# Column sums of 18 more attention groups on VectorE instead of TensorE, later folds, and quotients issued singly

## The chip, the core and the metric

The kernel runs on one core of a Trainium2 chip. A core has five engines with a queue of instructions each: TensorE (PE: matmuls, and PEld, its weight loads), VectorE (DVE), ScalarE (ACT), GpSimd (POOL) and SyncE (SP, which here issues DMAs). Each engine takes its own queue in order, and waits at an instruction until the semaphores that it names are set. The metric is the device time of one execution in microseconds (us). Before the change it is 3623.77 us, the median of 3 runs from 3623.32 to 3624.26.

## What is computed

Two attention layers over `x` of 8 x 32 x 32 x 512 (float32), each behind a group norm of 32 groups and with a residual. Layer 0 has 16 heads of 32, layer 1 has 4 heads of 128 and a bias from relative positions. Cut to what matters:

```python
def attention_layer_0(xn):                     # per batch: 1024 tokens x 512
    q, k, v = split(xn @ w_qkv)                # 16 heads of 32
    attn = softmax(einsum('bhid,bhjd->bhij', q * 32 ** -0.5, k), axis=-1)
    out = einsum('bhij,bhjd->bhid', attn, v)
    return merge(out) @ w_proj + b_proj

def attention_layer_1(xn):                     # 4 heads of 128
    scores = (xn @ Wq * 128 ** -0.5) @ (xn @ Wk).T + relative_positions
    return merge(softmax(scores) @ (xn @ Wv)) @ Wo

x = x + attention_layer_0(_gn(x))
x = x + attention_layer_1(_gn(x))
```

The softmax of layer 0 is what the change is about: the exponentials are multiplied with `v` first, and the result is divided by the sum of the exponentials afterwards.

## The kernel before

**Stages.** All work is in `quick_path` (L30). The kernel walks over the 8 batches and overlaps them. In stage b, `attention_0` of batch b (L859) is the leading strand, and `side_by_side` (L1611) places beside each of its steps some of the "rest": the output projection of layer 0 for batch b-1, that of layer 1 for batch b-2, the projections and the attention of layer 1 for batch b-1 (`attention_1`), loads, and the projections of layer 0 for batch b+1 (`before_0`). `side_by_side` counts costs in units of PE work, so that the rest is spread evenly over the 64 steps of the leading strand. `woven` (L1599) does the same on a smaller scale: it puts one step of a side strand after chosen steps of a main strand. Each strand is a Python generator, and a `yield` ends a step. The order written so is what a scheduler starts from when the program is built; it fixes the order of each engine's queue. `tc.issue_after(ins)` asks for an instruction not to be queued ahead of another, and `tc.keep_in_program_order` is for matmuls that may not be moved.

**Projections.** Matrix products with the weights are done with seven products in place of eight (`seven`, L506), with matmuls in four column strips of 32 (`by_columns`, L426, matmul L430). The names `x_`, `y_`, `z_` are its PSUM banks, and `a_`, `b_`, `p_` the partial results that ACT copies and DVE adds (L520, L528, L682, L685). `reader[0]`, `begun[0]` and `half_done[0]` hold the latest of certain adds, to which other work is tied.

**Attention of layer 0.** A batch has 8 groups: m (a set of 4 heads, in the order 0, 2, 1, 3) times h (a half of 512 queries). A group has 8 steps j over blocks of 128 keys:

- `front` (L878): 8 matmuls (L886) into the PSUM tile `ps`, four banks wide, of which there is one; then one exponential on ACT (L901) of 128 x 2048 elements into a slot of `e_room`.
- `back` (L904), one step behind: 4 matmuls (L912) add e times v into `acc`, and, but for the first step, DVE adds e to the group's running sum `esum` (L924).

`e_room` has three slots. Two take turns for the exponentials; the third holds the sum of the group, for which the first exponential's own slot is used. So the slot of the old group's sum is freed for exponentials when the group is finished, and the third exponential of the new group (j = 2) writes into it.

The 128 partitions of `esum` still have to be added up. There are two ways:

- `finish` (L930): four matmuls with `ones` (L934, 512 columns each) give the sums over partitions, spread over the strip; ACT copies them to SBUF (L764), DVE transposes in blocks of 32 (L766), takes the reciprocal (L781), checks it (L784) and spreads it by another transpose (L796); POOL multiplies `q` (where `acc` was put) with it (L770).
- `Apart` (L807): DVE transposes each of the four 512-column parts of `esum` (L826) and reduces each by 32 (L829) into a slot of `few_0`. Transposes 3 and 4 are tied behind `reader[0]`. For a tuple of groups, one `fold_up` (L837) of four small matmuls (L841) adds what is left, DVE inverts it, and each group has a `quotient`: a spread (L796) and POOL's multiplication (L857).

Which groups go the second way is told by `APART` (L26) and `apart_of` (L138): none in batch 0, (2, 3) in batch 1, (2, 3, 4) in batches 2 to 6, (3, 4) in batch 7. The tuple (2, 3, 4) is handed to the attention of layer 1 that runs beside it, which folds it with its own sums (`closing`) and issues its quotients among its own (`quotients`, woven into `before_0`).

**Attention of layer 1** (`attention_1`) has its scores by L1139, exponentials by L1142, its products by L1153 and adds on DVE (L1167, L1169); it has the sums of all its groups folded at once and its 8 quotients issued in pairs, each followed by one of `aside_0`.

Of the kernel before, what the change touches and what calls it, by code (L numbers as in the profile page):

```python
# [22 lines left out]

BLOCKS = 8

APART = [(2, 3, 4)]  # L26


@with_exitstack
def quick_path(  # L30
# [107 lines left out]
    def apart_of(b):  # L138
        if b == 1:
            return [(2, 3)] + APART[1:]  # L140
        return [] if b == 0 else [(3, 4)] if b == B - 1 else APART

    n_checks = B * CC * NH + 2 * 4 + B - 2
    n_checks -= sum(len(some) - 1 for b in range(B) for some in apart_of(b))
# [650 lines left out]
    def spread(su, rec):  # L795
        return nc.vector.transpose(  # L796
            su.rearrange("p (t c) -> p t c", c=32),
            rec.unsqueeze(2).to_broadcast([P, NB // 32, 32]),
        )
# [2 lines left out]
    e_room = mem.tile([P, 3, HB, NB], F32, tag="e0", name="e_room", bufs=1)  # L802
    turn, sum_at = [0, 1], [2]

    few_0 = mem.tile([P, HB, 3, NB // 32], F32, tag="few0", name="few_0", bufs=1)

    class Apart:  # L807


        def __init__(self, b, some):  # L810
            self.b, self.some = b, some
            self.groups = []
            self.width = len(some) * (NB // 32)

        def place(self, r):
            return few_0[:, r, : len(self.some), :]

        def take(self, m, h, esum, dst):
            at = len(self.groups)
            self.groups.append((m, h, dst))  # L820
            for r0 in range(0, HB, 2):
                turned = []
                for r in (r0, r0 + 1):
                    t = mem.tile([P, NB], F32, tag="rec", name=f"tu_0_{self.b}_{m}_{h}_{r}", bufs=2)
                    with tc.issue_after(reader[0].ins) if r0 else nullcontext():
                        nc.vector.transpose(t, esum[:, r, :])  # L826
                    turned.append(t)
                for r, t in zip((r0, r0 + 1), turned):
                    nc.vector.tensor_reduce(  # L829
                        few_0[:, r, at, :],  # L830
                        t.rearrange("p (t c) -> p t c", c=32),
                        axis=AX.X,
                        op=ALU.add,
                    )
                yield
# [16 lines left out]
        def quotient(self, i, behind=None):  # L852
            m, h, dst = self.groups[i]
            su = mem.tile([P, NB], F32, tag="rec", name=f"su_0_{self.b}_{m}_{h}", bufs=2)
            with tc.issue_after(behind.ins) if behind is not None else nullcontext():
                spread(su, few_0[:, 0, i, :])
            nc.gpsimd.tensor_tensor(dst, dst, su, op=ALU.mult)  # L857

    def attention_0(q, k, v, b, blocks=range(NT)):  # L859

        steps = [(m, h, j) for m in (0, 2, 1, 3) for h in range(NH) for j in blocks]
        state = {}
        aparts = {i: part for some in apart_of(b) for part in [Apart(b, some)] for i in some}

        def sums_apart(i, m, h, esum):
            part = aparts[i]
            together = i == 4 and b < B - 1
            if together:
                aside.append(part)
            yield from part.take(m, h, esum, q[m][:, h * NB : (h + 1) * NB])  # L870
            if together or i != part.some[-1]:
                return
            part.fold_up()
            for i in range(len(part.some)):
                yield
                part.quotient(i)

        def front(m, h, j):  # L878
            name = f"0_{b}_{m}_{h}_{j}"
            ps = wide_tile(f"ps_{name}")  # L880
            for i in range(2):

                some = slice(64 * i, 64 * i + 64)
                for r in range(HB):
                    rows = slice(r * D0, (r + 1) * D0)
                    nc.tensor.matmul(  # L886
                        ps[some, r, :],
                        k[m][rows, j * P + 64 * i : j * P + 64 * i + 64],
                        q[m][rows, h * NB : (h + 1) * NB],
                        start=True,  # L890
                        stop=True,
                    )
            at = turn.pop(0)
            if j == blocks[0]:

                turn.append(sum_at[0])
                sum_at[0] = at
            else:
                turn.append(at)
            e = e_room[:, at]  # L900
            exps[0] = nc.scalar.activation(e, ps, AF.Exp, scale=D0 ** -0.5)  # L901
            return e

        def back(m, h, j, e):  # L904
            name = f"0_{b}_{m}_{h}_{j}"
            if j == blocks[0]:
                state["acc"] = psum.tile([P, NB], F32, tag="acc", name=f"acc_{name}", bufs=1)
                state["first"] = e
            acc = state["acc"]
            for r in range(HB):  # L910
                c0 = (m * HB + r) * D0
                nc.tensor.matmul(  # L912
                    acc[r * D0 : (r + 1) * D0, :],
                    v[:, j, c0 : c0 + D0],
                    e[:, r, :],
                    start=(j == blocks[0]),
                    stop=(j == blocks[-1]),
                )
            if j == blocks[1]:
                state["esum"] = state["first"]  # L920
            if j != blocks[0]:

                with tc.issue_after(reader[0].ins) if beside_norm[0] else nullcontext():
                    summed[0] = nc.vector.tensor_add(state["esum"], state["esum"], e)  # L924
            if j != blocks[-1]:
                return
            nc.scalar.copy(q[m][:, h * NB : (h + 1) * NB], acc)
            state["ended"] = (m, h, state["esum"])

        def finish(m, h, esum):  # L930
            name = f"0_{b}_{m}_{h}"
            su = psum.tile([P, NB], F32, tag="acc", name=f"sums_{name}", bufs=1)
            for r in range(HB):
                nc.tensor.matmul(  # L934
                    su[r * D0 : (r + 1) * D0, :],
                    ones,
                    esum[:, r, :],
                    start=True,
                    stop=True,
                )  # L940
            normalise(q[m][:, h * NB : (h + 1) * NB], su, name)

        pending = None
        ended, ending = 0, []
        for at in steps:
            if "ended" in state:
                if ended in aparts:
                    ending.append(sums_apart(ended, *state.pop("ended")))
                else:
                    finish(*state.pop("ended"))  # L950
                ended += 1
            for part in ending:
                next(part, None)
            e = front(*at)
            if pending is not None:
                back(*pending)
            pending = (*at, e)
            yield 2
        for part in ending:
            run(part)  # L960
        back(*pending)
        yield 1
        finish(*state.pop("ended"))
# [113 lines left out]
    def attention_1(q, k, v, seeds, b, beside=0, final=False):  # L1077
# [161 lines left out]
            yield 0  # L1239

        def quotients():
            for i in range(H1 * NH):
                late = half_done if i // 2 % 2 == 0 else closed
                run(quotient(i, late[0], nc.gpsimd))
                if i % 2:
                    if aside_0 is not None and i // 2 < len(aside_0.some):
                        aside_0.quotient(i // 2, begun[0])
                    yield 0

        ends.append(closing())  # L1250
        if together:
# [347 lines left out]
    def woven(main, side, start, gap, places=(0,)):  # L1599

        for at, cost in enumerate(main):
            if at >= start and (at - start) % gap in places:
                cost += next(side, 0)
            yield cost
        yield from side

    def run(part):
        for _ in part:
            pass
# [36 lines left out]
    def later(part, *args):  # L1646

        yield from part(*args)
# [48 lines left out]
    for b in range(B + 1):  # L1697
# [69 lines left out]
        if coming is not None:  # L1767

            before = later(before_0, b + 1, coming, forms_0 if last is not None else None)
            if b + 2 < B:  # L1770
                n = len(ORDER)
                turning = later(turn_ahead, b + 2, states[b + 2], int(last is None))
                before = woven(before, turning, *((n - 1, n, (0, 4)) if last is None else (2 * n + 3, n, (0, 3))))
            if last is not None:
                before = woven(before, later(left.pop), 3, len(ORDER), (0, 3))
            rest.append(before if last is not None else woven(before, other_sums(), 2, 7))
            total += 3 * PRODUCT - PRODUCT // 2
        if b == 0:
# [502 lines left out]
```

## Time and profile before

| | |
|---|---|
| median of 3 runs | 3623.77 us (3623.32 to 3624.26) |
| the profiled execution, own time | 3626.2 us |
| its span, first to last instruction | 3624.4 us |
| mean granted TensorE clock | 0.999 |
| exponentials of layer 0 (L901) | 512 of 1879 ns |
| adds into the sum (L924) | 448, 2236 to 3393 ns, median 2292 |
| matmuls with `ones` (L934) | 360 in 45 groups, 51.2 us busy |
| fold matmuls (L841) | 56 in 7 folds, 192 to 230 ns |
| POOL's multiplications behind a fold (L857) | 19 of 3122 ns |
| POOL's multiplications behind `finish` (L770) | 45 of 1563 ns |

How the views are read: the first part of the page gives each engine's busy time, its share of the span and its instructions. The chain that ended last follows the work back from the last instruction to what released it. The groups by line have, in this order, the line, engine, operation, what it writes and reads, the count, the busy time and the mean of one in ns, and the idle time of the engine just before them with what ended it. The timeline has the start, the length, and in brackets the idle time before and its releaser. Neighbouring matmuls overlap in their records, so their starts tell more than their lengths.

The busy time of DVE, in stretches of 15 us around the ends of the sixth (1534.1 us) and seventh group (1573.6 us) of batch 3, is 12.90 (from 1515), 10.43, 14.98, 9.35, 11.99 and 11.60 us (to 1605). PE is busy 15.00 us in each.

### The profile page before, as it was taken

The page shows a single profiled execution, that of the slowest core. Times are in us where ns is not written, and L with a number is a line of the kernel's source. Part 1 is how long each engine was busy: PE and PEld are TensorE (multiplying, and loading weights), DVE is VectorE, ACT ScalarE, POOL GpSimd, SP SyncE. Part 2 cuts the span into 40 slices and gives each one's busy share as a digit, 9 for nine tenths or more (in the row PEclk, how much of TensorE's full clock was granted, in tenths as well). Part 3 has the DMA queues.
Part 4 walks back from the last instruction along what each step waited for, and adds up shares of the span by engine and source line. Part 5 has one row for each costly group of instructions (what it writes and reads, how often), then busy time and mean ns, then how long its engine had stood idle before and what let it go on. Part 6 is the DMA issues. An engine that isn't in the chain of part 4 may idle for free.

```text
span 3624.4 us, 80755 instructions
## 1 busy us (share of the span) xinstructions
PE 3604.8 (99%) x33786; PEld 1230.2 (34%) x33786; DVE 2573.9 (71%) x2807; ACT 1990.6 (55%) x2266; POOL 1399.2 (39%) x880
## 2 busy tenths in 40 slices
PE   9999999999999999999999999999999999999999
PEld 4232244232433234332343323433234232323343
DVE  6788656787667966679666796667966678667546
ACT  3555666446664466544665446654566545656254
POOL 1343055231552316523075230742318312166255
PEclk9999999999999999999999999999999999999999
DMA  6233164242643426344363433624336133324376
GB/s 192 73 111 104 44 175 137 64 145 68 187 126 89 131 66 195 110 112 112 84 195 90 135 97 101 186 74 139 85 101 203 55 101 79 103 91 158 97 200 155
DMA packets 577316, 431.96 MB, mean 119 GB/s; under 512 B 274320, under 2 KB 467632, under 8 KB 575920
## 3 DMA queue, kind: packets, MB, share of 16 engines
q1 hardware_dynamic: 567952, 411.05, 40.7%
q0 software_dynamic: 2608, 13.70, 1.0%
q8 instruction: 268, 4.39, 0.5%
q10 hardware_dynamic: 6384, 1.97, 0.2%
q14 instruction: 104, 0.85, 0.1%
HBM read 334.30 MB, written 92.27 MB: 118 GB/s over the span
## 4 chain that ended last, share of the span: by engine, by line
PE 96%; DVE 2%; ACT 1%; issue 1%; DMA 0%; POOL 0%; SPq 0%; DVEq 0%; ACTq 0%; POOLq 0%
PE ps L886 15%; PE acc L912 14%; PE ps L1139 12%; PE acc L1153 12%; PE y_v L430 5%; PE y_q L430 4%; PE y_k L430 4%; PE z_v L430 3%; PE x_v L430 3%; PE z_q L430 3%; PE x_k L430 3%; PE x_q L430 3%; PE z_k L430 3%; PE y_wp L430 2%; PE y_wo L430 2%; PE x_wp L430 2%
## 5 line engine op out<-in xcount | busy, mean ns | idle before, releaser
L901 ACT ACTIVATE e_room<-ps 128x2048 f32<-128x2048 f32 x512 | 962.0, 1879 | 749.8 <-PE ps L886 728.1
L924 DVE TENSOR_TENSOR e_room<-e_room 128x2048 f32<-128x2048 f32 x448 | 1093.4, 2441 | 375.2 <-ACT e_room L901 373.7
L1064 POOL TENSOR_TENSOR pos<-pos,columns 128x512 f32<-128x512 f32 x448 | 642.8, 1453 | 179.5 <-DMA pos<-pr 178.0
L886 PE MATMUL ps<-q,k 32*64 32x512 f32 x8192 | 594.0, 613 | 2.1 <-ACT e_room L901 2.0
L912 PE MATMUL acc<-e_room,v 128*32 128x512 f32 x4096 | 546.8, 604 | 0.0
L1139 PE MATMUL ps<-q,k 128*128 128x512 f32 x1024 | 527.3, 598 | 0.3 <-ACT ps L1073 0.3
L1153 PE MATMUL acc<-e,v 128*128 128x512 f32 x1024 | 523.9, 594 | 0.0
L1142 ACT ACTIVATE e<-ps 128x512 f32<-128x512 f32 x512 | 305.8, 597 | 316.9 <-PE ps L1139 308.8
L1169 DVE TENSOR_TENSOR es<-es,e 128x512 f32<-128x512 f32 x384 | 276.7, 721 | 285.1 <-ACT e L1142 282.4
L1153 PEld LDWEIGHTS acc<-e,v 128*128 128x128 f32 x1024 | 193.6, 190 | 248.1 <-issue 134.0
L1139 PEld LDWEIGHTS ps<-q,k 128*128 128x128 f32 x1024 | 191.0, 190 | 254.9 <-issue 229.7
L1073 ACT COPY ps<-pos 128x512 f32<-128x512 f32 x448 | 264.8, 592 | 0.4
L886 PEld LDWEIGHTS ps<-q,k 32*64 32x64 f32 x8192 | 123.1, 130 | 394.7 <-issue 201.2
L912 PEld LDWEIGHTS acc<-e_room,v 128*32 128x32 f32 x4096 | 81.4, 108 | 412.6 <-issue 366.2
L689 POOL TENSOR_TENSOR k<-b_k,p_k 128x512 f32<-128x512 f32 x32 | 49.4, 1544 | 426.6 <-ACT p_k L534 415.8
L770 POOL TENSOR_TENSOR q<-q,su 128x512 f32<-128x512 f32 x45 | 70.3, 1563 | 352.0 <-DVE su L796 328.0
L689 POOL TENSOR_TENSOR v<-b_v,p_v 128x512 f32<-128x512 f32 x32 | 51.8, 1620 | 358.6 <-ACT p_v L534 334.0
L689 POOL TENSOR_TENSOR q<-b_q,p_q 128x512 f32<-128x512 f32 x32 | 62.9, 1967 | 273.0 <-ACT p_q L534 258.5
L1110 POOL TENSOR_TENSOR q<-q,su 128x512 f32<-128x512 f32 x48 | 76.8, 1621 | 180.2 <-DVE su L796 180.0
L993 ACT COPY pos<-pp 32x512 f32<-32x512 f32 x128 | 104.9, 820 | 29.2 <-PE pp L984 27.9
L1167 DVE TENSOR_TENSOR es<-e,e 128x512 f32<-128x512 f32 x64 | 64.2, 1003 | 66.6 <-ACT e L1142 66.6
L1064 POOL TENSOR_TENSOR slots<-slots,columns 128x512 f32<-128x512 f32 x64 | 84.0, 1341 | 22.2 <-DMA slots<-pr 22.1
(246 smaller groups left out, 4613.6 us busy)
## 6 DMA issues: line engine op xcount, KB each, us to landing
pos<-pr SPq DMA_DIRECT2D x448, 256.0 KB, 3.5
w_qkv<-ws_qkv SPq DMA_DIRECT2D x168, 128.0 KB, 2.7
x1T<-d SPq DMA_DIRECT2D x32, 512.0 KB, 5.2
d<-x1T SPq DMA_DIRECT2D x32, 512.0 KB, 3.6
pc<-pos SPq DMA_DIRECT2D x32, 512.0 KB, 6.8
pr<-pos SPq DMA_DIRECT2D x32, 512.0 KB, 7.9
columns<-pc SPq DMA_DIRECT2D x64, 256.0 KB, 4.4
x2T<-d SPq DMA_DIRECT2D x32, 512.0 KB, 6.0
```

What stands on the lines that cost most here:

```text
L430: ins = nc.tensor.matmul(out[columns, :], weights[:, columns], moving, start=start, stop=stop, skip_group_check=open_sum,)
L689: nc.gpsimd.tensor_tensor(self.dst[1][1], s(b), s(p7), op=ALU.add)
L886: nc.tensor.matmul(ps[some, r, :], k[m][rows, j * P + 64 * i : j * P + 64 * i + 64], q[m][rows, h * NB : (h + 1) * NB], start=True, stop=True,
L901: exps[0] = nc.scalar.activation(e, ps, AF.Exp, scale=D0 ** -0.5)
L912: nc.tensor.matmul(acc[r * D0 : (r + 1) * D0, :], v[:, j, c0 : c0 + D0], e[:, r, :], start=(j == blocks[0]), stop=(j == blocks[-1]),)
L924: summed[0] = nc.vector.tensor_add(state["esum"], state["esum"], e)
L1064: nc.gpsimd.tensor_tensor(self.rows[i], self.rows[i], self.columns[i // NT], op=ALU.add)
L1073: self.copied = nc.scalar.copy(ps, rows)
L1139: scored[0] = nc.tensor.matmul(ps, k[h][:, keys], q[:, h, queries], start=False, stop=True, skip_group_check=True)
L1142: exps[0] = nc.scalar.activation(e, ps, AF.Exp, scale=1.0 / math.sqrt(D1))
L1153: nc.tensor.matmul(acc, v[:, j, h * D1 : (h + 1) * D1], e, start=(j == 0), stop=(j == NT - 1),)
L1169: added[0] = nc.vector.tensor_add(state["esum"], state["esum"], e)
```

## The change

More groups go the second way: in batch 0 two tuples, (0, 1, 2) and (3, 4, 5); in batches 1 to 6 groups 5 and 6 as a tuple of their own. That is 18 groups and 8 folds more. Batch 7 keeps its tuple. A tuple that isn't handed to layer 1's attention gets one more `yield` between its last reduction and its fold. `few_0` has four slots where it had three; the tuple (5, 6) uses the last two, in reverse order. The buffers of the transposes of batch 0 and of the tuple (5, 6) are taken from the tag `columns` and no more from `rec`. In layer 1's attention, the quotients are issued one by one, those of `aside_0` first, all tied behind `half_done` or `closed`, and at four places in seven where it was two. In the changed kernel the lines lie 2 to 14 further down: `spread` is L798, the transposes L837, the reductions L840, the fold's matmuls L852, POOL's multiplication L868, the scores L898, the products with v L924, the add L936, the `ones` matmuls L946.

```diff
--- before.py
+++ after.py
@@ -23,7 +23,7 @@
 
 BLOCKS = 8
 
-APART = [(2, 3, 4)]
+APART = [(2, 3, 4), (5, 6)]
 
 
 @with_exitstack
@@ -138,7 +138,9 @@
     def apart_of(b):
         if b == 1:
             return [(2, 3)] + APART[1:]
-        return [] if b == 0 else [(3, 4)] if b == B - 1 else APART
+        if b == 0:
+            return [(0, 1, 2), (3, 4, 5)]
+        return [(3, 4)] if b == B - 1 else APART
 
     n_checks = B * CC * NH + 2 * 4 + B - 2
     n_checks -= sum(len(some) - 1 for b in range(B) for some in apart_of(b))
@@ -802,7 +804,7 @@
     e_room = mem.tile([P, 3, HB, NB], F32, tag="e0", name="e_room", bufs=1)
     turn, sum_at = [0, 1], [2]
 
-    few_0 = mem.tile([P, HB, 3, NB // 32], F32, tag="few0", name="few_0", bufs=1)
+    few_0 = mem.tile([P, HB, 4, NB // 32], F32, tag="few0", name="few_0", bufs=1)
 
     class Apart:
 
@@ -810,10 +812,16 @@
         def __init__(self, b, some):
             self.b, self.some = b, some
             self.groups = []
+            self.tag = "columns" if some[0] == 5 or b == 0 else "rec"
+
+            self.base = 2 if some[0] == 5 else 0
+            self.slots = [self.base + i for i in range(len(some))]
+            if some[0] == 5:
+                self.slots.reverse()
             self.width = len(some) * (NB // 32)
 
         def place(self, r):
-            return few_0[:, r, : len(self.some), :]
+            return few_0[:, r, self.base : self.base + len(self.some), :]
 
         def take(self, m, h, esum, dst):
             at = len(self.groups)
@@ -821,13 +829,16 @@
             for r0 in range(0, HB, 2):
                 turned = []
                 for r in (r0, r0 + 1):
-                    t = mem.tile([P, NB], F32, tag="rec", name=f"tu_0_{self.b}_{m}_{h}_{r}", bufs=2)
+
+                    t = mem.tile(
+                        [P, NB], F32, tag=self.tag, name=f"tu_0_{self.b}_{m}_{h}_{r}", bufs=2
+                    )
                     with tc.issue_after(reader[0].ins) if r0 else nullcontext():
                         nc.vector.transpose(t, esum[:, r, :])
                     turned.append(t)
                 for r, t in zip((r0, r0 + 1), turned):
                     nc.vector.tensor_reduce(
-                        few_0[:, r, at, :],
+                        few_0[:, r, self.slots[at], :],
                         t.rearrange("p (t c) -> p t c", c=32),
                         axis=AX.X,
                         op=ALU.add,
@@ -853,7 +864,7 @@
             m, h, dst = self.groups[i]
             su = mem.tile([P, NB], F32, tag="rec", name=f"su_0_{self.b}_{m}_{h}", bufs=2)
             with tc.issue_after(behind.ins) if behind is not None else nullcontext():
-                spread(su, few_0[:, 0, i, :])
+                spread(su, few_0[:, 0, self.slots[i], :])
             nc.gpsimd.tensor_tensor(dst, dst, su, op=ALU.mult)
 
     def attention_0(q, k, v, b, blocks=range(NT)):
@@ -864,12 +875,13 @@
 
         def sums_apart(i, m, h, esum):
             part = aparts[i]
-            together = i == 4 and b < B - 1
+            together = i == part.some[-1] == 4 and b < B - 1
             if together:
                 aside.append(part)
             yield from part.take(m, h, esum, q[m][:, h * NB : (h + 1) * NB])
             if together or i != part.some[-1]:
                 return
+            yield
             part.fold_up()
             for i in range(len(part.some)):
                 yield
@@ -1239,13 +1251,15 @@
             yield 0
 
         def quotients():
-            for i in range(H1 * NH):
+
+            for i in range(H1 * NH + (len(aside_0.some) if aside_0 is not None else 0)):
                 late = half_done if i // 2 % 2 == 0 else closed
-                run(quotient(i, late[0], nc.gpsimd))
-                if i % 2:
-                    if aside_0 is not None and i // 2 < len(aside_0.some):
-                        aside_0.quotient(i // 2, begun[0])
-                    yield 0
+                apart = len(aside_0.some) if aside_0 is not None else 0
+                if i < apart:
+                    aside_0.quotient(i, late[0])
+                else:
+                    run(quotient(i - apart, late[0], nc.gpsimd))
+                yield 0
 
         ends.append(closing())
         if together:
@@ -1772,7 +1786,7 @@
                 turning = later(turn_ahead, b + 2, states[b + 2], int(last is None))
                 before = woven(before, turning, *((n - 1, n, (0, 4)) if last is None else (2 * n + 3, n, (0, 3))))
             if last is not None:
-                before = woven(before, later(left.pop), 3, len(ORDER), (0, 3))
+                before = woven(before, later(left.pop), 3, len(ORDER), (0, 1, 3, 4))
             rest.append(before if last is not None else woven(before, other_sums(), 2, 7))
             total += 3 * PRODUCT - PRODUCT // 2
         if b == 0:
```

## The prediction

> **What bounds the kernel now.** I read the page from the top: busy shares, the chain that ended last, the costliest groups. TensorE (PE) works almost without a gap and nearly the whole chain is PE. So only what takes PE's time, or makes PE wait, is worth anything; work removed from the others is free until PE waits for it.
>
> ```profile
> PE 3604.8 (99%) x33786; PEld 1230.2 (34%) x33786; DVE 2573.9 (71%) x2807; ACT 1990.6 (55%) x2266; POOL 1399.2 (39%) x880
> ...
> PE 96%; DVE 2%; ACT 1%; issue 1%; DMA 0%; POOL 0%; SPq 0%; DVEq 0%; ACTq 0%; POOLq 0%
> ...
> L901 ACT ACTIVATE e_room<-ps 128x2048 f32<-128x2048 f32 x512 | 962.0, 1879 | 749.8 <-PE ps L886 728.1
> L924 DVE TENSOR_TENSOR e_room<-e_room 128x2048 f32<-128x2048 f32 x448 | 1093.4, 2441 | 375.2 <-ACT e_room L901 373.7
> ```
>
> The reader is to see that the exponential (L901) and the adding of its result (L924) mostly wait for PE. The list of groups by line then prices what a group's end costs: the `ones` matmuls (L934), and, in the groups already summed apart, transposes (L826) and reductions (L829).
>
> ```profile
> L934 PE MATMUL sums<-e_room,ones 128*32 128x512 f32 x360 | 51.2, 596 | 0.4 <-DVE e_room L924 0.4
> L826 DVE STREAM_TRANSPOSE tu<-e_room 128x512 f32<-128x512 f32 x76 | 49.3, 687 | 0.3
> L829 DVE TENSOR_REDUCE few<-tu 128x16 f32<-128x512 f32 x76 | 47.4, 658 | 0.0
> L764 ACT COPY su<-sums 128x512 f32<-128x512 f32 x45 | 26.4, 586 | 69.6 <-PE sums L934 69.6
> ```
>
> Last the timeline of one group end that is to change (sixth group of batch 3), on PE, then on VectorE (DVE); columns are start, length, operation.
>
> ```profile
> 1532.81 1.47 PE L430 MATMUL x_q<-x0T,w_qkv 128*32 128x512 f32 x12
> 1534.10 1.05 PE L934 MATMUL sums<-e_room,ones 128*32 128x512 f32 x8
> 1535.08 1.11 PE L886 MATMUL ps<-q,k 32*64 32x512 f32 x16
> ```
>
> ```profile
> 1538.21 3.19 DVE L924 TENSOR_TENSOR e_room<-e_room 128x2048 f32<-128x2048 f32 x1 [0.38 <-ACT e_room L901]
> 1541.32 0.68 DVE L528 TENSOR_TENSOR b_q<-y_q,p_q 128x512 f32<-128x512 f32 x1
> 1541.92 1.29 DVE L796 STREAM_TRANSPOSE su<-few 128x512 f32<-128x512 f32 x2
> 1544.70 0.71 DVE L796 STREAM_TRANSPOSE su<-few 128x512 f32<-128x512 f32 x1 [1.49 <-POOL q L1110]
> ```
>
> **The change, part by part.** *1. Removed from PE.* 18 of the 45 groups lose their `ones` matmuls: six of batch 0 and groups 5 and 6 (counted from 0) of batches 1 to 6. The two sets of four take 0.98 us from their start to the next `ps` (1534.10 to 1535.08). In single matmuls, the last product starts 0.43 us before the sums, and where products go straight over to `ps` the step is 0.54: 0.43 + 0.98 - 0.54 = 0.87 us (0.86 at group 6). A fold's records are 0.21 us (L841, 56 of them), but its four sit side by side: 0.215 + 0.175 from start to start against 0.33 without, about 0.06 us. Batches 1 to 6: 6 x (1.73 - 0.06) = 10.0 us off. In batch 0 the six are worth 0.87, 0.84, 0.97, 0.87 and twice 1.99 (around 222 and 250 us the sums also split a `ps` into 1 and 7), 7.5 us.
>
> *2. Added to DVE.* Per group 4 x 0.687 + 4 x 0.658 = 5.38 us, against a transpose, reciprocal and check of 1.23 saved; with a share of the fold's inversion (0.8 us a pair) about +4.5. ACT loses 18 copies of 0.586, off the path. Cover: DVE's idle time, (1 - 0.71) x 453 = 131 us a batch for 9 us more. Over the whole this is nothing, but around group 5 it is tight: DVE is busy 10.43 of 15 us from 1530, and 14.98 of 15 from 1545. There I put the stall.
>
> *3. Group 5's sum is late.* The old group's sum holds one of three `e_room` slots, and the new group's third exponential (step 2) writes it. All four transposes must be over by then. In the order in which the changed kernel queues DVE, batches 2 to 6 have transposes 1 and 2, then the next group's first add (L924), a `b_q` add and two quotient spreads, and only then transposes 3 and 4 (that the last two follow a reader, L826's wait, is in the code). On the times of before: first exponential of the second step ends 1537.31 without the sums, +2.29 add, +0.68 `b_q`, +1.29 two spreads, +1.3 two transposes and switching = 1542.9. The third exponential would start at 1540.9 and the `ps` behind it has 0.7 us of slack (1.88 us of exponential against some 2.5 of other PE work). PE waits 2.0 - 0.7, I take 1.25 us, x 5 = 6.2 us. Nearest rows bound it: 0 if the spreads come earlier (they also wait for POOL, which may shift them out), 2.3 us each if the add takes 3.19 as it did here. Batch 1's order has the four transposes together, and group 6's are done (1577.4) before its exponential is ready (about 1579): nothing. Behind the waiting exponential stand ACT's evictions of products, then PE.
>
> [...] In the rows the add takes 2.29 alone and 3.19 beside a POOL multiplication; that multiplication 1.28 alone and 3.3 beside an add. [...]
>
> *4. Batch 0's folds stand too early.* In the changed PE order the fold of (0,1,2) follows the last `acc` of group 2 after only three product matmuls, and that of (3,4,5) follows its last `acc` at once, two or three steps ahead of where the program issues them. PE takes them in order, and they need DVE's last add (2.3 to 3.2), two transposes and one or two reductions (2.0 to 2.7). `ps` (1.04 us) and `acc` (0.9) run meanwhile. So PE waits about 3.8 us (1.5 to 4.5) at the first and 2.9 at the second. Further: half-filled sets of four beside the split folds 1.3, a late exponential slot after group 1 behind three `f_xn`/`x0T` operations of 1.2 to 2.3 us at 122 to 130 us 0.9, four fillers missing between two `ps` 0.7, the folds 0.1. Sum 9.7 us against 7.5 off: +2.2 us, between -4 (waits at their low ends, no extras) and +7 (all at the upper ends).
>
> *5. The rest.* Folds one step later: batch 1's (2,3) and batch 7's (3,4) had no PE idle before them (the L841 rows show none), so 0. Quotients singly: same counts of spreads and POOL products; POOL has 61% idle. Their spreads wait in DVE's queue for a free buffer (15.7 us in all before); with `aside_0`'s 3.1 us products first, POOL would have freed those of this window by 1533, earlier than they are asked for. 0, between -3 (all five windows gain the 0.6 us the DVE queue lost to POOL at 1528.6) and +3 (the opposite). Half of the transposes share a buffer with `columns` (64 loads, SP's queue): the next such load comes only with the next batch's biases; nothing is queued against it in time, 0.
>
> *Sum.* -10.0 + 6.2 + 2.2 + 0 = -1.6 us. The profiled execution took 3626.2 (span 3624.4 and 1.8 around it): 3624.6 by it. The median of the runs is 2.4 lower, 3623.8, so **3622.2 us**.
>
> **The rivals.** *A, full gain.* The late transposes and the early folds find cover: group 5's stall 0, batch 0 at -4: -14, 3610 us. For it: 29% of DVE idle, 375 us of it waiting for exponentials. Against: the order of the queues is fixed, and a slot needed at 1540.9 is free at 1542.9. Under half of it (-7.3) it is "faster".
>
> *B, DVE becomes the bound after group 5.* Window 1545 to 1560 has no DVE time left. Group 5 adds 5.38 - 1.93 (normalising, its spread moved later) = 3.4 us just ahead of it. If none is absorbed, PE waits 3.4 five times: -10.0 + 17 + 2.2 = +9.2, **3633 us**, slower. It decides from 3.0 us a batch on. Against: 2.64 us of idle DVE at 1533.3 to 1536 is where transposes 1 and 2 go.
>
> *C, the folds don't wait.* If the order of the folds in batch 0 costs nothing, batch 0 gives its 7.5: -10.0 + 6.2 - 7.0 = -10.8, 3613 us. Against: their operands come at the end of DVE work that is in the same queue as the add.
>
> **How the numbers follow.** What can be told from no change here is about 0.2%, 7.25 us: faster below 3616.5, slower above 3631.0. Forecast (both stalls of the computed kind, 3616.5 to 3630) 0.59, A 0.15, C 0.11, B 0.15. Faster is A and C less the part of C that stays within the bound: 0.25; within: 0.60; slower: B, 0.15. The range runs from A's 3610 to just short of B's, 3632; it leaves out the outer half of A and B.
>
> **What would show it.** L946 (the `ones` matmuls) with 216 records instead of 360, 18 copies fewer on ACT, L837 and L840 at 148 each (76 + 72). PE idle before `ps` with the exponential as its releaser shortly after group 5 in batches 2 to 6, 1.2 us each: absent, A or C; 3 us, B. PE idle before `sums` L852 in batch 0, about 3.8 and 2.9 us, with the reduction as releaser: absent, step 4 is wrong. Rising PE idle anywhere else, above all with DVE over 95% in the 15 us after group 5, would make the prediction wrong.

## The result and the profile after

The changed kernel takes 3630.73 us (median of 20 runs, 3627.21 to 3636.26), the kernel before 3623.66 us (20 runs, 3623.24 to 3626.84): 7.1 us more, a ratio of 1.0019 with a 95% interval of 1.0012 to 1.0025. The forecast was 3622.2 us, 1.6 us less than before. The profiled execution took 3630.39 us (span 3628.6). The runs lie two and a half times as wide apart as before (9.1 us against 3.6), and that turned out to be part of the answer.

The page of the changed kernel: busy times, then the chain.

```profile
PE 3591.0 (99%) x33706; PEld 1229.3 (34%) x33706; DVE 2626.9 (72%) x2903; ACT 1979.9 (55%) x2248; POOL 1393.0 (38%) x880
...
PE 92%; DVE 5%; ACT 1%; issue 1%; POOL 0%; DMA 0%; SPq 0%; DVEq 0%; ACTq 0%; POOLq 0%
```

PE is busy 13.8 us less, and the span is longer all the same: DVE's share of the chain went from 2 to 5%. The groups by line say that the work moved as it was meant to (216 records of the `ones` matmuls, 148 transposes and reductions), and the waits say who stands still. Columns of the second fence: who waited for whom, us in total, times, longest.

```profile
L837 DVE STREAM_TRANSPOSE tu<-e_room 128x512 f32<-128x512 f32 x148 | 96.6, 685 | 0.7
L840 DVE TENSOR_REDUCE few<-tu 128x16 f32<-128x512 f32 x148 | 91.9, 658 | 0.0
...
L946 PE MATMUL sums<-e_room,ones 128*32 128x512 f32 x216 | 31.4, 596 | 1.2 <-DVE e_room L936 1.2
```

```profile
PE ps L898 <- ACT e_room L913: 9.6, 13, 1.1
...
PEld sums L852 <- DVE few L840: 8.3, 4, 4.0
...
PE sums L852 <- DVE few L840: 6.0, 3, 3.1
```

So PE waits at the folds (L852) for the reductions, and before `ps` for the exponential. Where the time goes is read best by setting the first exponential of every group beside that of before (after minus before, us):

| place | first profile | second profile (e1) |
|---|---|---|
| batch 0, group 0 | +0.28 | +0.14 |
| batch 0, group 3 | -1.44 | -1.58 |
| batch 0, group 4 | +3.62 | +4.59 |
| batch 0, group 7 | +4.39 | +8.21 |
| batch 1, group 1 | +6.95 | +10.77 |
| batch 4, group 1 | +5.63 | +9.33 |
| batch 7, group 1 | +4.30 | +7.99 |
| end | +4.20 | +7.08 |

Batch 0 and the start of batch 1 cost 6.7 and 10.6 us; batches 1 to 6 give back 0.43 to 0.46 us each in both profiles, but for 0.53 us in batch 1 of the second.

The timeline on PE of the group of batch 3 that the prediction showed, and on DVE:

```profile
1545.76 1.11 PE L898 MATMUL ps<-q,k 32*64 32x512 f32 x16
1546.81 1.07 PE L924 MATMUL acc<-e_room,v 128*32 128x512 f32 x8
1547.69 1.90 PE L432 MATMUL y_q<-f_xn,w_qkv 128*32 128x512 f32 x16
1550.73 1.12 PE L898 MATMUL ps<-q,k 32*64 32x512 f32 x16 [1.14 <-ACT e_room L913]
```

```profile
1543.42 2.29 DVE L936 TENSOR_TENSOR e_room<-e_room 128x2048 f32<-128x2048 f32 x1 [2.77 <-ACT e_room L913]
1545.63 0.68 DVE L530 TENSOR_TENSOR b_q<-y_q,p_q 128x512 f32<-128x512 f32 x1
1546.23 1.29 DVE L798 STREAM_TRANSPOSE su<-few 128x512 f32<-128x512 f32 x2
1547.45 1.26 DVE L837 STREAM_TRANSPOSE tu<-e_room 128x512 f32<-128x512 f32 x2
```

The reader sees the sequence of the prediction's step 3: add, `b_q`, two spreads, and only then transposes 3 and 4; PE stands idle until the exponential behind them is through. The records overlap; from the starts of single matmuls (the step from one to the next, less the 0.43 us that a set of products takes) the idle is 1.31 us, in batches 1 to 6. Idle times below are counted in this way unless they stand in a quoted line.

And PE in batch 0, at the fold of (0, 1, 2):

```profile
155.95 1.03 PE L432 MATMUL y_q<-f_xn,w_qkv 128*32 128x512 f32 x6
159.62 0.27 PE L852 MATMUL sums<-few,fold 128*32 128x48 f32 x2 [2.63 <-DVE few L840]
160.21 0.27 PE L852 MATMUL sums<-few,fold 128*32 128x48 f32 x2 [0.32 <-DVE few L840]
160.31 1.40 PE L432 MATMUL z_q<-x0T,w_qkv 128*32 128x512 f32 x2
161.64 2.01 PE L898 MATMUL ps<-q,k 32*64 32x512 f32 x16
```

Behind the idle something happens that was in no step: the sixteen matmul records of one `ps` take 2.01 us and not 1.11. The windows of these stretches give the granted clock (the figure after the five engines' busy times), here first of the first profile, then of the second:

```profile
150.00:160.00 10.00, 7.26 (x76) 1.68 (x72) 9.86 (x8) 4.80 (x4) 9.68 (x5) 1.00 0.43 147
160.00:170.00 10.00, 9.79 (x88) 2.38 (x88) 7.98 (x14) 3.77 (x2) 4.21 (x2) 0.83 0.30 118
...
250.00:260.00 10.00, 6.75 (x92) 2.12 (x84) 9.35 (x15) 4.23 (x3) 1.46 (x3) 1.00 0.66 246
```

```profile
160.00:170.00 10.00, 9.96 (x76) 2.37 (x80) 6.85 (x11) 2.90 (x2) 3.31 (x2) 0.69 0.31 120
...
250.00:260.00 10.00, 6.88 (x66) 1.79 (x64) 8.49 (x12) 2.78 (x4) 2.10 (x2) 0.74 0.64 221
```

In the window of ten microseconds at or behind an idle of about 3 us PE runs on a clock of 0.83, 0.69 or 0.74, and once, after the same idle, on 1.00.

### The profile page after: what moved, and what is told of

Same layout as the page of the kernel before. It is cut to its first block, busy times and chain, and to the rows that moved or that the text cites. A ratio compares the mean times of both kernels' runs of the same rounds, so it can differ in the third digit from the quotient of the medians.

```text
span 3628.6 us, 80679 instructions
## 1 busy us (share of the span) xinstructions
PE 3591.0 (99%) x33706; PEld 1229.3 (34%) x33706; DVE 2626.9 (72%) x2903; ACT 1979.9 (55%) x2248; POOL 1393.0 (38%) x880
## 4 chain that ended last, share of the span: by engine, by line
PE 92%; DVE 5%; ACT 1%; issue 1%; POOL 0%; DMA 0%; SPq 0%; DVEq 0%; ACTq 0%; POOLq 0%
PE ps L898 14%; PE acc L924 13%; PE ps L1151 12%; PE acc L1165 12%; PE y_v L432 4%; PE y_k L432 4%; PE y_q L432 4%; PE x_v L432 3%; PE z_v L432 3%; PE x_k L432 3%; PE x_q L432 3%; PE z_q L432 3%; PE z_k L432 3%; PE y_wp L432 2%; DVE e_room L936 2%; PE y_wo L432 2%
## 5 line engine op out<-in xcount | busy, mean ns | idle before, releaser
L936 DVE TENSOR_TENSOR e_room<-e_room 128x2048 f32<-128x2048 f32 x448 | 1085.3, 2422 | 391.3 <-ACT e_room L913 389.7
L1076 POOL TENSOR_TENSOR pos<-pos,columns 128x512 f32<-128x512 f32 x448 | 653.1, 1480 | 173.8 <-DMA pos<-pr 171.8
L898 PE MATMUL ps<-q,k 32*64 32x512 f32 x8192 | 591.3, 613 | 9.6 <-ACT e_room L913 9.6
L924 PE MATMUL acc<-e_room,v 128*32 128x512 f32 x4096 | 546.7, 605 | 0.0
L898 PEld LDWEIGHTS ps<-q,k 32*64 32x64 f32 x8192 | 122.7, 130 | 395.5 <-issue 195.2
L924 PEld LDWEIGHTS acc<-e_room,v 128*32 128x32 f32 x4096 | 81.4, 108 | 413.0 <-issue 372.4
L868 POOL TENSOR_TENSOR q<-q,su 128x512 f32<-128x512 f32 x37 | 77.3, 2106 | 229.6 <-DVE su L798 229.6
L691 POOL TENSOR_TENSOR q<-b_q,p_q 128x512 f32<-128x512 f32 x32 | 52.1, 1627 | 291.8 <-ACT p_q L536 291.7
L772 POOL TENSOR_TENSOR q<-q,su 128x512 f32<-128x512 f32 x27 | 46.2, 1710 | 235.0 <-DVE su L798 223.9
L1122 POOL TENSOR_TENSOR q<-q,su 128x512 f32<-128x512 f32 x48 | 83.3, 1753 | 121.2 <-DVE su L798 121.2
```

Of the source, the lines that this page charges most:

```text
L691: nc.gpsimd.tensor_tensor(self.dst[1][1], s(b), s(p7), op=ALU.add)
L898: nc.tensor.matmul(ps[some, r, :], k[m][rows, j * P + 64 * i : j * P + 64 * i + 64], q[m][rows, h * NB : (h + 1) * NB], start=True, stop=True,
L924: nc.tensor.matmul(acc[r * D0 : (r + 1) * D0, :], v[:, j, c0 : c0 + D0], e[:, r, :], start=(j == blocks[0]), stop=(j == blocks[-1]),)
L1076: nc.gpsimd.tensor_tensor(self.rows[i], self.rows[i], self.columns[i // NT], op=ALU.add)
```

## The experiments

All are compared with the kernel before on the same chip; its median was 3623.9 to 3624.0 us each time.

**e1: the changed kernel once more.**

> The changed kernel once more, for a second profile and for its spread (its runs went from 3627.2 to 3636.3 us, those of before from 3623.2 to 3626.8). Theory (loss in batch 0, fixed queues): about 3630.5 us; group ends of batches 1 to 6 lie exactly as in the first profile (1.31 us of PE idle each, -0.44 us a batch), and what differs between the two profiles lies in batch 0 and at the end. Rival (the loss is spread over all batches by chance): the differences appear in every batch.

3629.82 us (11 runs, 3627.94 to 3633.35), ratio 1.0015 (1.0006 to 1.0024). The table above has its profile: batches 1 to 6 alike, all differences between the two in batch 0 and at the end. The theory holds. Over the 31 runs of e1 and the first series the time follows the mean granted clock: 3627.2, 3627.4 and 3627.9 us at 1.000, 3633.6 and 3636.3 us at 0.997.

**e2: batch 0 undone.**

```diff
         if b == 0:
-            return [(0, 1, 2), (3, 4, 5)]
+            return []
```

> Batch 0 keeps the sums by ones; groups 5 and 6 of batches 1 to 6, later folds and single quotients stay. Theory (the loss is batch 0's folds and DVE's lateness there): six batches of -0.44 us, -2.6 us against before, about 3621 us (3619 to 3624), spread as narrow as before. Rival (later folds, quotients or the end of the kernel cost the time): still 3 us or more slower than before, 3627 us or more, with the wide spread.

3622.46 us (3621.82 to 3625.73), ratio 0.9996 (0.9987 to 1.0005). Group 1 of batch 7 begins 2.78 us earlier than before, 0.44 to 0.53 us for each of six batches. So the loss goes with batch 0's two tuples.

**e3: only batch 0.**

```diff
-APART = [(2, 3, 4), (5, 6)]
+APART = [(2, 3, 4)]
```

> Only batch 0's two tuples, with later folds and single quotients; groups 5 and 6 by ones. Theory: +6.7 us, about 3630 us (3628 to 3634), and the wide spread if that comes from batch 0. Rival: within 2 us of before.

3636.03 us (8 runs, 3632.78 to 3637.80), ratio 1.0030 (1.0020 to 1.0041): 12.1 us, above the expected 6.7 and outside the 3628 to 3634 us, at mean clocks of 0.997 to 0.999. Its profile has +8.49 us by group 1 of batch 1 and nothing more up to batch 7. The wide spread (5.0 us in 8 runs) points to batch 0. By the medians e2 and e3 together (10.7 us) are more than the whole change (5.9 and 7.1 us in its two series). In the profiles they are not: at group 1 of batch 7, -2.78 and +8.41 make +5.63 us, between the +4.30 and +7.99 of the whole. That e3's other runs lost more by the clock than its profiled one fits their low clocks, but no profile shows it.

**e4: the wait at group 5 taken away.** As e2, and

```diff
-                    with tc.issue_after(reader[0].ins) if r0 else nullcontext():
+                    with tc.issue_after(reader[0].ins) if r0 and self.base == 0 else nullcontext():
                         nc.vector.transpose(t, esum[:, r, :])
```

> As e2, and transposes 3 and 4 of the tuple (5, 6) are no more tied behind a reader: all four stand ahead of the next group's first add, so the sum's slot is free before the third exponential. Theory (the 1.31 us is the wait for that slot): it goes in all six batches, -1.73 + 0.06 = -1.67 each, -10 us against before, 3613.5 us (3612 to 3616). Rival (DVE is full there, and the wait only moves to a later add or exponential): between -2 and -5 us, 3619 to 3622 us.

3615.46 us (3614.97 to 3616.01), ratio 0.9975 (0.9965 to 0.9985): 8.5 us faster than before and 14 us faster than e1 on the same chip. Its DVE timeline at group 5 of batch 3, where all four transposes now stand ahead of the add:

```profile
1530.17 1.24 DVE L840 TENSOR_REDUCE few<-tu 128x16 f32<-128x512 f32 x2
1531.32 1.29 DVE L837 STREAM_TRANSPOSE tu<-e_room 128x512 f32<-128x512 f32 x2
1532.54 1.24 DVE L840 TENSOR_REDUCE few<-tu 128x16 f32<-128x512 f32 x2
1534.20 2.29 DVE L936 TENSOR_TENSOR e_room<-e_room 128x2048 f32<-128x2048 f32 x1 [0.42 <-ACT e_room L913]
```

PE has no idle there (15.00 of 15 us busy from 1530 and from 1545), and each of batches 2 to 6 is worth -1.66 us: the 1.73 - 0.06 that step 1 worked out. The wait did not move on. Against the -0.44 us of e2 this puts the price of the 1.31 us of idle at 1.22 us: about 0.1 us of it is the change from products to `ps` (0.54 us against 0.43 in the rows of before), which PE spends without a wait too.

**e5, e9, e10: longer waits at group 5.** As e2, with transpose 4 (in batch 2 transpose 3) repeated, `DOSE` times by batch; e9 is e5 again, e10 has more repeats. Each is a single profiled execution (3635.1, 3633.0 and 3642.8 us).

```diff
+DOSE = [0, 0, 1, 1, 2, 3, 5, 0]      # e10: [0, 0, 4, 5, 6, 7, 8, 0]
...
-                        nc.vector.transpose(t, esum[:, r, :])
+                        for _ in range(1 + more):
+                            nc.vector.transpose(t, esum[:, r, :])
```

> As e2 (batch 0 by ones), but group 5's late transposes are repeated, with nothing else changed in the result, so that the third exponential waits longer: by the DVE rows 1.3 us of PE idle in batch 1, 1.95 in batch 2, 2.6 in batch 3, 3.2 in batch 4, 3.9 in batch 5, 5.2 in batch 6. Theory (a long idle of PE, wherever it lies, lowers the granted clock right behind it): the windows of 10 us behind these places show 1.00 at 1.3 and 1.95 us and under 0.9 from some length between 2.6 and 3.9 us on, and the time lost between group 5 and group 7 exceeds the idle by 1 to 3 us there. Rival (the low clock belongs to the first 300 us, whatever the idle): 1.00 in all six.

> e5 once more, the same kernel, for a second profile. Theory (a window of fixed length that runs free of the program decides whether an idle lowers the clock, so chance decides between 2.4 and 3.2 us): the idles are the same to 0.1 us as in e5 (1.9, 2.5, 2.4, 3.1, 2.9 us), and other ones of the four long idles are followed by a low clock than in e5 (there the last alone). Rival (length alone decides): again the last alone, 0.85 and 0.81.

> As e5 with more repeats: by the rows some 3.5, 4, 4.5, 5 and 5.5 us of PE idle in batches 2 to 6. Theory (idle of PE lowers the clock behind it): a window of 5 us under 0.9 behind at least four of the five, and none behind the 1.3 us of batch 1. Rival (it needs the first 300 us or the kernel's end): at most one.

| batch | e5 and e9: idle us | clock behind (e5; e9) | e10: idle us | clock behind |
|---|---|---|---|---|
| 1 | 1.31 | 1.00; 1.00 | 1.31 | 1.00 |
| 2 | 1.90 | 1.00; 1.00 | 2.89 | 1.00 |
| 3 | 2.49 | 1.00; 1.00 | 2.93 | 0.66 |
| 4 | 2.40 | 1.00; 1.00 | 3.26 | 0.79, 0.87 |
| 5 | 3.15 | 1.00; 1.00 | 0.66 + 2.45 | 0.66 |
| 6 | 2.92 | 0.85, 0.81; 0.90, 0.76 | 0.65 + 2.78 | 0.72, 0.94 |

(Clock of the windows of 5 us behind the idle; the scheduler filled part of the longer waits with products, so that the idles came out shorter than expected.) Two of e10's windows, before and behind the idle of 2.93 us in batch 3:

```profile
1545.00:1550.00 5.00, 2.51 (x18) 0.48 (x10) 4.86 (x8) 1.66 (x1) 0.74 (x1) 1.00 0.18 52
1550.00:1555.00 5.00, 4.73 (x36) 1.07 (x40) 4.63 (x5) 2.10 (x2) 1.75 (x2) 0.66 0.00 0
```

So an idle of PE that an edit makes longer brings a low clock behind it at 1.5 to 2.9 ms into the kernel too, and none does at 1.9 us or less here. The fall belongs to the idle and not to the kernel's start. In batch 3 of e10 the way from group 6 to 7 took 4.44 us more than before: 0.87 off for the sums and 2.93 of idle leave 2.4 us. Half a clock for 3.41 us, as its record has it, is 1.7 of them; the rest was not traced. e10 came out as expected (four of five); e5 and e9 did not in full: 3.15 us of idle passed at 1.00, and in e9 the same idle had the low clock as in e5. So length alone does not decide.

The kept traces show what else does. In narrow windows the clock is 1.00 or 0.50 and nothing between, and it changes only at the bounds of steps 3.413 us long: the trace of before has 0.50 for 6.83 us from 3189.23 us, that of the changed kernel for 3.41 us from 160.82 us, and in e10 it falls at 1550.78, 1997.93, 2445.07 and 2892.22 us, each 131 steps behind the last. Where the steps lie against the program is not the same in two executions: behind the wait at the first fold of batch 0, which begins at 156.82 us in the first profile of the changed kernel and at 156.69 us in e1, the clock falls at 160.82 and at 159.27 us. Here is the wait at the second fold of batch 0 cut into such steps, first profile, then e1:

```profile
249.57:252.98 3.41, 1.84 (x24) 0.16 (x8) 3.34 (x4) 2.35 (x2) 1.34 (x2) 1.00 0.45 167
252.98:256.39 3.41, 1.92 (x30) 0.68 (x30) 3.41 (x7) 0.00 (x0) 0.00 (x0) 1.00 0.53 192
```

```profile
251.43:254.85 3.42, 1.11 (x16) 0.16 (x8) 3.39 (x3) 2.35 (x2) 0.67 (x2) 1.00 0.55 230
254.85:258.26 3.41, 2.61 (x22) 1.19 (x30) 3.41 (x7) 0.00 (x0) 0.00 (x0) 0.50 0.51 169
```

PE (the first figure behind the length) waits 3.2 and 3.3 us. In the first profile a bound of steps splits the wait into 1.7 and 1.5 us, and the clock stays at 1.00; in e1 2.5 us of it lie in one step, and the clock is 0.50 for the next two. So it is in all fourteen profiles, up to the last 25 us, wherever dense matmuls stand on both sides of the idle: 2.19 us or more of idle within one step (the 2.19 us in batch 6 of e10) was followed by 0.50, 1.90 us or less was not. The 0.50 lasts one step or two (3.41 or 6.83 us), of which the half, up to 1.7 or 3.4 us, is my estimate of what is lost.

**e6: batch 0's folds two steps later on PE**, with all of the change kept.

```diff
+                with tc.issue_after(last_acc[0].ins) if self.b == 0 else nullcontext():
                     ins = nc.tensor.matmul(
                         su[r * D0 : (r + 1) * D0, :],
...
-                nc.tensor.matmul(
+                last_acc[0] = nc.tensor.matmul(
                     acc[r * D0 : (r + 1) * D0, :],
```

> The changed kernel with batch 0's folds queued behind the latest matmuls with v, two steps later on PE. Theory (their early place makes PE idle for some 6.5 us, and the clock falls behind it): both idles of 2.8 and 3.2 us before the folds go, the granted clock is 1.00 in all windows of the first 330 us, the spread of the runs is that of before (under 4 us), and the time is 3630.2 - 6.5 - 2 to 4 = 3620 to 3622 us. Rival (the time in batch 0 is lost by DVE's lateness anyhow, and the wait moves on): 3627 us or more.

3626.73 us (3625.01 to 3629.76), ratio 1.0007 (0.9998 to 1.0016): between the two, and nearer the rival; the runs lie 4.8 us apart, not under 4. The idle before the folds is gone, and the clock is 1.00 in all windows of the first 330 us. But PE now waits elsewhere, for adds of the projections that stand behind transposes in DVE's queue, and for exponentials:

```profile
251.25 1.48 PE L432 MATMUL y_v<-w_qkv,f_xn 128*32 128x256 f32 x18 [2.35 <-DVE b_v L530]
```

```profile
249.36 1.24 DVE L841 TENSOR_REDUCE few<-tu 128x16 f32<-128x512 f32 x2
250.51 0.68 DVE L530 TENSOR_TENSOR b_v<-y_v,p_v 128x512 f32<-128x512 f32 x1
```

Between 140 and 330 us PE's records leave 8.2 us idle, against 9.2 in the changed kernel and 0.1 before. So the folds' place was where the waiting showed, and DVE's lateness is what lies behind it: in e6 DVE is busy 29.17 of the 30 us from 150 and 27.80 of the 30 us from 240, where PE waits.

**e7: e6 and e4 together.**

> e6 and e4 together: all 18 groups on DVE, folds of batch 0 late, all four transposes of groups 5 and 6 ahead of the next add. Theory: e6 less six waits of 1.31 us, 3612 to 3614 us, which would be 1 to 3 us faster than e4. Rival (batch 0 has no DVE time for it): slower than e4's 3615.5 us, by 2 us or more.

3619.76 us (3617.94 to 3622.90), ratio 0.9987 (0.9978 to 0.9996): the rival. Batch 0 has no DVE time for the six sums at either place of the folds, and e4, which leaves it alone, is 4.3 us faster. Here the same idle as in e6 (2.50 us at 248 us) was followed by half a clock: in e7 it lies in one step of 3.413 us, in e6 it is split into 1.3 and 1.2 us. The tie that e4 takes away stays in batch 0, but it holds nothing up at the folds: in the changed kernel the four transposes stand together there (from 157.69 and from 252.54 us), behind adds.

**e8: no group moved**, only the later folds, the single quotients and the other buffers (the edits of e2 and e3 together).

> No group more on DVE: only the fold one step later, the quotients singly and the other buffers. Theory (these cost nothing up to batch 7): the exponentials of batches 0 to 6 lie where they lay before within 0.3 us; the -3.0 us at the end of batch 7 and the +1.9 us behind it that all four kernels so far show come from here, together 3622 to 3624 us. Rival (they come from the groups 5 and 6): batch 7 and the end as before, 3623.9 us.

3624.26 us (3623.55 to 3627.34), ratio 1.0002 (0.9993 to 1.0011): these parts cost nothing that shows, and the exponentials of batches 0 to 6 lie within 0.3 us of before. The -3.0 us at the end of batch 7 is there, but it does not come from these parts, as the expectation had it: its cause is in the profile of before. Windows of before, then of e8:

```profile
3185.00:3190.00 5.00, 3.96 (x22) 0.93 (x16) 4.31 (x3) 3.03 (x4) 5.00 (x2) 0.92 0.94 346
3190.00:3195.00 5.00, 5.00 (x13) 1.33 (x14) 1.06 (x1) 1.51 (x3) 3.57 (x4) 0.50 0.50 179
3195.00:3200.00 5.00, 5.00 (x24) 1.18 (x24) 1.65 (x2) 2.96 (x3) 2.54 (x2) 0.89 0.14 52
```

```profile
3185.00:3190.00 5.00, 3.96 (x16) 0.68 (x8) 4.02 (x3) 3.28 (x4) 5.00 (x2) 1.00 0.94 367
3190.00:3195.00 5.00, 4.83 (x26) 1.54 (x25) 0.69 (x1) 2.95 (x4) 3.84 (x4) 1.00 0.61 192
```

The profiled execution of before had half a clock here for 6.8 us, behind an idle of 1.2 us among sparse matmuls (8 records in the step of 3.413 us that has the idle, 57 and 56 in the two ahead of it). The idle is 1.2 us here in all fourteen profiles, and the clock fell in six of them; what decides between them stays open. The times of before fall in two heaps: of the 20 runs in the first series 18 lie from 3623.2 to 3624.3 us and two at 3626.7 and 3626.8; the profiled execution, at 3626.2 us, is by its time of the upper kind. Behind batch 7 e8's profile loses 0.9 us against before, the other kernels' up to 2.9 us; this was not cleared up.

**e11, e12: e4 with the quotients in pairs as before, and e4 without the extra `yield` ahead of the fold.**

```diff
             if together or i != part.some[-1]:
                 return
-            yield
             part.fold_up()
```

> e4 with the quotients in pairs as before. Theory (quotients singly are worth nothing by themselves): as e4, 3615.5 us within 1.5 us. Rival (with groups 5 and 6 on DVE the pairs hold up the third exponential): 1 us a batch more, 3620 us or more.

> e4 without the step between the last reduction and the fold. Theory (DVE is done in time in batches 1 to 7): as e4, 3615.5 us within 1 us, with no PE idle before the folds of (5, 6). Rival (the fold then waits for its reductions as in batch 0): 0.5 to 2 us of PE idle before each of six folds, 3618 us or more.

3615.19 us (ratio 0.9974, 0.9964 to 0.9984) and 3615.32 us (0.9975, 0.9966 to 0.9984): both as e4. Neither edit is needed for the gain.

## Why the prediction was wrong

The sum said 1.6 us less, and the kernel takes 7.1 us more. That 3630.73 us still lies in the stated range (3610 to 3632) is owed to the width of the range: the sign was wrong.

- *Step 1, off PE: right.* e4 shows -1.66 us a batch against 1.67.
- *Step 3, group 5: right in mechanism and size.* 1.31 us of idle, of which 1.22 count, against 1.25. The add took 2.29 us, as the sum had it. The wait was put into five batches and is in six: batch 1 waits too, at group 6. Batches 1 to 6 give -2.7 us in place of -3.8.
- *Step 5, the rest at nothing: right* (e8, e11, e12).
- *Step 4, batch 0: this is the step that failed.* "Sum 9.7 us against 7.5 off: +2.2 us" measured +6.7, +8.3 and +10.6 in three profiles (changed kernel, e3, e1). The waits at the folds were nearly right: PE idles 2.8 us, and 0.3 more between the fold's halves, at the first and 3.2 us at the second (3.8 and 2.9 were said). Two things were put at nothing. One is waits that no term names, for adds that come late on DVE: 1.04, 0.75 and 0.98 us at 205, 245 and 310 us, 2.8 us together. The other is a price for idling: behind both folds the granted clock can fall, for another 1.7 us (a window of 10 us at 0.83) to 6.9 us (e1: 0.4 + 3.1 + 2.6 + 0.8 from its four low windows). In the first profile 2.8 and 1.7 make 4.5 us, what +6.7 is above +2.2. This match is partly luck: the 0.9 us of a late slot at 122 to 130 us did not come (the first exponential of group 2 is 0.87 us earlier by the sums, from +0.28 to -0.59), and the half-filled sets, the fillers and the 7.5 us off were not measured one by one. Since the fall of the clock depends on where an execution's steps lie (behind the second fold 1.00 in the first profile, 0.50 in e1), it is part of the spread of the runs as well. The fastest runs, at a clock of 1.000, are 4.0 us above the fastest of before; the median is 7.1 above. About 3 of the 7 us are the clock, an estimate from these two.
- *The cause in batch 0* was read too narrowly, as the folds' place. e6 and e7 show that DVE does not take the six sums in time at a later place either: the wait moves to exponentials and `b_v`. DVE's mean share did not tell this (72 of 90.6 us there before the change, from 90.6 us on, and 85 of 90.6 from 1177.8 us on). Fewer groups of batch 0, or another order of DVE's other work there, were not tried. Rival C (7.5 us saved, of which its sum took 7.0) is refuted by the same two; A's share at group 5 was there to be had, but only by another order (e4). Rival B did not occur: PE never waited 3 us at group 5, and DVE absorbed the sums in batches 1 to 6.
- *The base of the sum.* 2.4 us between the profiled execution and the median were carried along as a constant. By the profiles they were an event, the half clock at 3190 us, and windows of 5 us would have shown it before the change. Read there, it would have told that idling can cost more than its length: 1.2 us of idle stood ahead of 6.83 us at 0.50.

## What to carry to other kernels

An idle of the engine that sets the time was not worth its length alone here: behind 2.19 us or more of it in one step of 3.413 us PE went on at a clock of 0.50 for 3.41 or 6.83 us, up to 1.7 or 3.4 us more by my estimate, the half of these lengths. So after a pause of PE look at the granted clock in narrow windows behind it. Work may be moved to an engine with idle time only if its result is not needed before that idle time comes: the same sums cost nothing where DVE had slack before the next use of the slot (-1.66 us a batch in e4), and more than they saved in batch 0 (+6.7 and +10.6 us in the two profiles of the changed kernel). A stall that a fixed queue order makes could be computed here from the rows, at group 5 to a tenth of a microsecond (1.25 us against 1.31 of idle) and at the folds to less than one (3.8 and 2.9 us against 3.1 and 3.2), and the one at group 5 was removed by taking away one tie (e4).

## What the runs showed of the hardware

The clock that TensorE is granted was 1.00 or 0.50 in narrow windows and changed only at the bounds of steps of 3.413 us (the trace of before: 0.50 for 6.83 us from 3189.23 us; the changed kernel: for 3.41 us from 160.82 us; e10: four falls, each 131 steps behind the last). Up to the last 25 us, it fell to 0.50 for one step or two (3.41 or 6.83 us) behind idles between dense matmuls with 2.19 us or more in one step (e10, batch 6, had the 2.19 us), never behind those with 1.90 us or less in one, and in six of fourteen profiles, before among them, behind an idle of 1.2 us among sparse matmuls. Where the steps lie against the program differed between executions: behind the wait at batch 0's first fold the clock fell at 160.82 us in the first profile of the changed kernel and at 159.27 us in e1.
